# The second graph's channel sums turned on TensorE and laid in node order

## The chip, the core and the metric

The kernel runs on one core of a Trainium2 chip. The metric is the device time of one launch in microseconds (us). A core has five engines that work side by side, each through its own queue in program order: TensorE (PE; its weight loads are listed as PEld), VectorE (DVE), ScalarE (ACT), GpSimd (POOL) and SyncE (SP), which here only issues DMAs. Engines wait for one another by semaphores. All data are float32.

## The reference

Sixteen graphs of 1024 nodes with 256 channels share one adjacency matrix. Layer 0 normalises the nodes, weights the adjacency by the differences of the nodes' channel sums, and attends with what comes out as queries; layer 1 is a graph convolution with two batch norms. What matters here is the weighting:

```python
h = jnp.maximum(_layernorm(x, axis=-1), 0.0)
fea = jnp.transpose(h, (0, 2, 1))
c_adj = jnp.mean(fea, axis=1)
diff = c_adj[:, None, :] - c_adj[:, :, None]
A = jnp.abs(jnp.abs(jax.nn.sigmoid(diff) - 0.5) - 0.5) * 2.0
A_s = (A + jnp.transpose(A, (0, 2, 1))) * 0.5
Wg = adj[None, :, :] * A_s
g = jax.nn.relu(jnp.einsum('bcn,bnm->bcm', fea, Wg) * para.reshape(1, C, N))
# g gives the queries; h @ kv_w gives keys and values; 4 heads of 64
x = x + softmax_attention(q, k, v)
# layer 1: norm, adjacency aggregation, linear, batch norm, relu, linear, batch norm
```

`A_s[n, m]` depends only on the absolute difference of two nodes' channel sums: it is 1 - tanh(|difference of their means| / 2). So for each graph the kernel needs, for all pairs of nodes n (on partitions) and m (along the free dimension), the absolute difference of the sums, a tanh and a product with `adj`.

## The kernel before, in words

A graph's 1024 nodes are laid out as 8 tiles of 128 partitions (`P` = 128, `NT` = 8), node n = t * 128 + p. The channel sums of graph b, a by-product of the norm's relu (L341), lie in `csum`, 128 partitions by 8: partition p, column t. The weighting needs them also as a row of 1024 along the free dimension, the same on each partition. That row is `cbc`.

- `differences(b)` (from L401) makes `cbc`. For graph 0 it is made on chip (`columns_of` L201, `broadcast_row` L212 and L213), in the order of the nodes. For all other graphs `csum` is written to a DRAM buffer `csum_d` (L414) and read back as a broadcast to all partitions (L415), both on SP's queue. The write goes partition by partition, so `cbc` holds element p * 8 + t for node t * 128 + p, and a view with step 8 puts it right.
- `weigh(b)` then works through eight tiles `w` of 128 x 1024, each covering two node tiles and half of the m's: two ACTIVATEs (L450, absolute value of `csum` minus `cbc`, 512 elements each, read through the view of `cbc`), a tanh (L458) over the 1024, and a product with `adj` on DVE (L437). `adj` tiles are loaded by SP (L183) into a ring of three buffers.
- `transposed` (L396 and L399) turns the normalised nodes for the key and value products; `keys_values` (L171 as `pk` and `pv`, copies at L624 and L641) and `plain_queries` (L171 as `pg`, L604, L607) make keys, values and queries. `plain_queries` serves graphs 0 and 1. All these products, and the transposes, take turns in two PSUM banks (`bank`, tag `mm`).
- `attention` runs over all graphs in steps of two score tiles: scores (L882) into two PSUM buffers, an exponential (L890), the value products (L923) one step later, and sums of the exponentials on DVE (L909 and L912).

The order is written out by hand (`manual_schedule`). Between two attention steps of graph b, `attention` takes pieces from a generator, `background(b)`, as long as their costs stay below what is due by then. A piece is mostly one or two products with what belongs to them; the costs only steer how many pieces come after each step. Every engine runs its instructions in the order in which the pieces issue them. The background of graph 0 begins with `differences(1)`, issued after the scores and exponentials of step 0 and before those of step 1. Then come the transposes of graph 1 at the top of the next two steps, key products with the weighting of graph 1 woven in (two slots of weighting for each piece), the norm of graph 2, `plain_queries(1)`, and, from its fifth and seventh piece, `graph()` (GpSimd prepares seven combinations of the adjacency in DRAM, `aht_d`, for layer 1) and `degrees()` (L226 to L240, `at` tiles loaded by SP at L217 into the same three buffers as `adj`). After that `differences(2)` and the rest.

The background of the later graphs weights graph b + 1 or b + 2 beside the attention in the same way. The weighting of graph 0 is done before the attention begins.

The buffer `s1` (128 x 4 x 128, one copy) is used in `degrees()` for the masked diagonal (L234), and later for the sums of quarters in the queries and in layer 1.

Of the kernel before, what the change touches and what calls it, by code (L numbers as in the profile page):

```python
# [10 lines left out]
F32 = mybir.dt.float32  # L11
# [6 lines left out]
P = 128  # L18
# [5 lines left out]
def gnn_two_layers_kernel(  # L24
# [12 lines left out]
    nc = tc.nc  # L37
    B, N, C = x.shape
    H1 = w1_t.shape[1]
    NT = N // P  # L40
# [14 lines left out]
    ident = const.tile([P, P], F32, name="ident")  # L55
# [16 lines left out]
    csum_d = [dram.tile([N], F32, name=f"csum_d{b}") for b in range(B)]  # L72
# [23 lines left out]
    def layers(shifted):  # L96
# [9 lines left out]
        p1 = st.enter_context(tc.tile_pool(name=f"p1_{kind}", bufs=1))  # L106
# [15 lines left out]
        csums, cbcs, weighted, weighers = {}, {}, {}, {}  # L122
# [41 lines left out]
        def bank(name):  # L164
            return ps_mm.tile([P, FB], F32, tag="mm", name=name)
# [30 lines left out]
        def columns_of(col, name):  # L196

            cbs = []
            for g in range(NT // 4):
                cb = py.tile([P, 4, P], F32, tag="y", name=f"cb_{name}_{g}")  # L200
                nc.vector.tensor_copy(  # L201
                    cb, col[:, 4 * g : 4 * g + 4].unsqueeze(2).to_broadcast([P, 4, P])
                )
                cbs.append(cb)
            return cbs

        def broadcast_row(dst, cbs, name):

            for g, cb in enumerate(cbs):
                pt = bank(f"cbp_{name}_{g}")  # L210
                for j in range(4):
                    nc.tensor.transpose(pt[:, j * P : (j + 1) * P], cb[:, j, :], ident)  # L212
                nc.scalar.copy(dst[:, g * FB : (g + 1) * FB], pt)  # L213
# [8 lines left out]
        row, diag, col, deg, tmp_deg, dinv = (deg_sm[:, i, :] for i in range(6))  # L222
# [178 lines left out]
        def differences(b):  # L401


            cbc = p1.tile([P, N], F32, tag="cbc", name=f"cbc_{b}")
            cbcs[b] = (
                cbc.rearrange("p (t q) -> p t q", t=NT)
                if b == 0
                else cbc.rearrange("p (q t) -> p t q", t=NT)
            )
            weighers[b] = weigh(b)  # L410
            if b == 0:
                broadcast_row(cbc, columns_of(csums[b], f"c{b}"), f"c{b}")
                return
            nc.sync.dma_start(out=csum_d[b].rearrange("(p t) -> p t", p=P), in_=csums[b])  # L414
            nc.sync.dma_start(  # L415
                out=cbc, in_=csum_d[b].rearrange("(o n) -> o n", o=1).to_broadcast([P, N])
            )

        def weigh(b):


            csum, cbc = csums[b], cbcs[b]
            made = weighted[b] = []
            adjs = []

            def load():
                q, th = divmod(len(adjs), NP)
                adjs.append(load_adj(q, th, f"adj_{b}_{q}_{th}"))

            load()  # L430
            for slot in range(2 * NH * NP + 1):
                i, odd = divmod(slot, 2)
                q, th = divmod(i, NP)
                if not odd and i > 0:

                    w, a = made[i - 1], adjs[i - 1]
                    nc.vector.scalar_tensor_tensor(w, w, 1.0, a, op0=ALU.add, op1=ALU.mult)  # L437
                    if b == 0:
                        q, th = divmod(i - 1, NP)
                        nc.vector.tensor_reduce(  # L440
                            rows[:, q, th * TH : (th + 1) * TH], a, AX.X, ALU.add
                        )
                if not odd and i < NH * NP:
                    q, th = divmod(i, NP)
                    if i + 1 < NH * NP:
                        load()
                    w = p8.tile([P, TH, FB], F32, tag="w", name=f"w_{b}_{q}_{th}")
                    made.append(w)
                    for t in range(TH):
                        nc.scalar.activation(  # L450
                            w[:, t, :].rearrange("p (t q) -> p t q", q=P),
                            cbc[:, q * NT // NH : (q + 1) * NT // NH],
                            AF.Abs,
                            bias=csum[:, th * TH + t : th * TH + t + 1],
                            scale=-1.0,
                        )
                if odd:
                    nc.scalar.activation(made[i], made[i], AF.Tanh, scale=-0.5 / C)  # L458
                yield 0.0
# [307 lines left out]
        def summed(b):  # L767
            yield from Norm(b, True).all()
            differences(b)
            yield 0.0  # L770
# [15 lines left out]
        def background(b):  # L786

            if b == 0:
                differences(1)
                for k in range(CC):  # L790
                    yield TOP
                    transposed(1, k)
                    yield 1.0
                w, products, norm = weighers[1], keys_values(1), Norm(2, True).all()
                yield from weave(
                    islice(products, 4), (0, double(islice(w, 8))), (0, islice(norm, 4))
                )
                yield from weave(
                    plain_queries(1), (0, norm), (0, w), (5, graph()), (7, degrees())
                )  # L800
                differences(2)
                yield from islice(products, 2)
                yield from prepare(2, products)
                return
# [627 lines left out]
```

## Time and profile before

| | |
|---|---|
| time, median of 3 runs | 2615.71 us (2615.10 to 2615.84) |
| time of the profiled execution | 2615.69 us |
| span of the profiled execution, first to last instruction | 2613.6 us |
| mean granted TensorE clock | 0.990 |
| ScalarE busy | 1468.9 us of the span |
| L450, all graphs | 256 instructions, 293.7 us of ScalarE |
| write of the sums (L414), issue to landing | 1.4 us median, 1.4 to 7.4 |
| broadcast back (L415), issue to landing | 4.4 us median, 4.2 to 4.9 |

In a timeline each line has the start in us, the duration, engine, line, operation, what is written and read with its shapes, how many instructions were merged, and in brackets how long the engine stood idle before it and for whom. A shape such as 64*128 64x512 on a TensorE row is the stationary operand by the moving one. In the groups by line, busy us and mean ns of one instruction stand after the first bar, idle time after the second. Matmul ends are modelled, so short overlaps of neighbouring rows mean nothing.

### The profile page before, as it was taken

To read this page: it belongs to the slowest core of one execution; us is meant where nothing else is said; L and a number is where in the kernel's file an instruction comes from. 1 tells how busy PE (TensorE), PEld (TensorE's weight loads), DVE (VectorE), ACT (ScalarE), POOL (GpSimd) and SP (SyncE) were. 2 spreads that over 40 slices of the span, in tenths; PEclk is the share of its full clock that TensorE was granted. 3 is DMA by queue.
4 is the path that set the end of the run, shared out by engine and by line. 5 is a ranking of instruction groups with operands and counts; after the bars stand their busy time and mean duration, and the time that the engine had idled before them with its cause. 6 is when DMAs were issued, how large, how long until landed. Compare 5 with 4: busy or idle time off the path is not lost. (4 is left out here: it accounts for less than half of the span.)

```text
span 2613.6 us, 31371 instructions
## 1 busy us (share of the span) xinstructions
PE 2525.8 (97%) x11626; PEld 931.8 (36%) x11626; DVE 1824.7 (70%) x2837; ACT 1468.9 (56%) x2033; POOL 393.6 (15%) x456
## 2 busy tenths in 40 slices
PE   7899999999999999999999999999999999999994
PEld 3333333333333333333333333333333333334443
DVE  4668686767768686868677676868686766657774
ACT  6875564647474645656474747465565634335543
POOL 1550100010101001000001010000100001026653
PEclk9999999999999999999999999999999999999997
DMA  4554324152524342241524243433325242355459
GB/s 158 178 197 145 121 81 162 61 189 77 181 81 153 101 151 95 97 157 55 188 73 181 85 153 109 145 101 113 138 63 180 64 166 104 109 191 224 169 198 365
DMA packets 131043, 363.46 MB, mean 139 GB/s; under 512 B 15425, under 2 KB 32321, under 8 KB 124737
## 3 DMA queue, kind: packets, MB, share of 16 engines
q1 hardware_dynamic: 110272, 282.70, 31.5%
q0 software_dynamic: 20608, 78.66, 7.9%
q8 instruction: 94, 1.54, 0.3%
q14 instruction: 69, 0.56, 0.1%
HBM read 286.79 MB, written 74.51 MB: 138 GB/s over the span
## 5 line engine op out<-in xcount | busy, mean ns | idle before, releaser
L890 ACT ACTIVATE p<-sc 128x1024 f32<-128x1024 f32 x512 | 495.2, 1020 | 450.8 <-PE sc L882 450.3
L912 DVE TENSOR_TENSOR acc<-acc,p 128x1024 f32<-128x1024 f32 x384 | 472.4, 1230 | 144.7 <-ACT p L890 123.2
L882 PE MATMUL sc<-q,k 64*128 64x512 f32 x2048 | 509.0, 615 | 8.8 <-ACT p L890 8.8
L923 PE MATMUL o<-p,v 128*64 128x512 f32 x2048 | 495.9, 605 | 0.0
L171 PE MATMUL pg<-w,h_a 128*64 128x512 f32 x1600 | 357.9, 592 | 4.4 <-DVE q L604 2.5
L171 PE MATMUL pa<-aht,h_b 128*64 128x512 f32 x1536 | 345.4, 594 | 3.5 <-ACT h_b L341 3.4
L882 PEld LDWEIGHTS sc<-q,k 64*128 64x128 f32 x2048 | 175.8, 186 | 330.9 <-issue 285.4
L450 ACT ACTIVATE w<-cbc,csum 128x512 f32<-128x512 f32 x256 | 293.7, 1199 | 0.0
L171 PE MATMUL py<-at,w 128*64 128x512 f32 x1024 | 234.0, 600 | 8.4 <-ACT ht L399 7.1
L437 DVE SCALAR_TENSOR_TENSOR w<-w,adj 128x1024 f32<-128x1024 f32 x128 | 157.2, 1228 | 118.8 <-ACT w L458 114.6
L923 PEld LDWEIGHTS o<-p,v 128*64 128x64 f32 x2048 | 124.1, 136 | 250.3 <-issue 247.2
L171 PEld LDWEIGHTS pg<-w,h_a 128*64 128x64 f32 x1600 | 114.7, 137 | 233.2 <-issue 215.2
L738 POOL DMA_DIRECT2D y_d<-y x128 | 70.8, 553 | 797.3 <-ACT y L737 789.5
L171 PEld LDWEIGHTS pa<-aht,h_b 128*64 128x64 f32 x1536 | 111.2, 137 | 217.5 <-issue 208.9
L737 ACT ACTIVATE y<-py,vec 128x512 f32<-128x512 f32 x128 | 87.6, 684 | 143.5 <-PE py L171 120.4
L741 DVE BATCH_NORM_STATS2 stats<-y 128x6 f32<-128x512 f32 x128 | 85.6, 687 | 80.7 <-ACT y L737 80.6
L458 ACT ACTIVATE w<-w 128x1024 f32<-128x1024 f32 x128 | 135.2, 1056 | 1.7
L512 DVE TENSOR_TENSOR w<-w,w 128x1024 f32<-128x1024 f32 x112 | 132.8, 1216 | 1.5
L341 ACT ACTIVATE h_b<-x,lnsm_b 128x256 f32<-128x256 f32 x128 | 70.4, 608 | 110.7 <-DVE lnsm_b L330 110.7
L93 POOL TENSOR_SCALAR lnsm_b<-mv_b 128x4 f32<-128x4 f32 x32 | 12.2, 381 | 790.9 <-DVE mv_b L319 790.9
L171 PEld LDWEIGHTS py<-at,w 128*64 128x64 f32 x1024 | 72.5, 138 | 163.3 <-issue 130.8
L171 PE MATMUL pk<-ht,kvw_f 128*64 128x512 f32 x512 | 116.8, 599 | 2.5 <-ACT ht L399 1.5
(155 smaller groups left out, 2778.8 us busy)
## 6 DMA issues: line engine op xcount, KB each, us to landing
aht<-aht_d SPq DMA_DIRECT2D x224, 512.0 KB, 6.3
adj<-in_adj_dram SPq DMA_DIRECT2D x128, 512.0 KB, 4.5
y_d<-y POOLq DMA_DIRECT2D x128, 256.0 KB, 2.6
yin_f<-y_d SPq DMA_DIRECT2D x32, 1024.0 KB, 6.3
x<-in_x_dram SPq DMA_DIRECT2D x32, 512.0 KB, 5.2
para<-in_para_dram SPq DMA_DIRECT2D x64, 256.0 KB, 3.9
x_d<-x POOLq DMA_DIRECT2D x16, 1024.0 KB, 10.3
xo_f<-x_d SPq DMA_DIRECT2D x32, 512.0 KB, 8.2
```

Of the source, the lines that this page charges most:

```text
L171: nc.tensor.matmul(dst[r], left[:, r], right, start=start, stop=stop)
L437: nc.vector.scalar_tensor_tensor(w, w, 1.0, a, op0=ALU.add, op1=ALU.mult)
L450: nc.scalar.activation(w[:, t, :].rearrange("p (t q) -> p t q", q=P), cbc[:, q * NT // NH : (q + 1) * NT // NH], AF.Abs, bias=csum[:, th * ...
L458: nc.scalar.activation(made[i], made[i], AF.Tanh, scale=-0.5 / C)
L512: nc.vector.tensor_sub(block(i)[part], block(x)[part], block(y)[part])
L737: nc.scalar.activation(y, made, AF.Identity, bias=b1[:, j : j + 1])
L738: nc.gpsimd.dma_start(out=y1_d[i][:, j, :], in_=y)
L741: nc.vector.bn_stats(stats1[:, j, i, :], y)
L882: nc.tensor.matmul(sc[:, e, :], ks[b][k][r, m * P : (m + 1) * P], qs[b][k][r, f * FB : (f + 1) * FB], start=True, stop=True,)
L890: nc.scalar.activation(pr, sc, AF.Exp)
L912: nc.vector.tensor_add(self.acc, self.acc, pr)
L923: nc.tensor.matmul(self.o[r, :], vs[b][k][:, m, r], pr[:, e, :], start=(m == 0), stop=(m == NT - 1),)
```

## The change

Only graph 1 is treated differently, and only in `differences`. Its `csum` (128 x 8) is turned by TensorE into a PSUM bank as 8 x 128, copied by ScalarE to a row tile in the buffer `s1`, and this is written to `csum_d`, in eight runs of 128 floats, node by node. The broadcast back is the same instruction as before. The view of `cbc` is then the one of graph 0, with step one. Graphs 2 to 15 keep the old way.

```diff
             cbcs[b] = (
                 cbc.rearrange("p (t q) -> p t q", t=NT)
-                if b == 0
+                if b <= 1
                 else cbc.rearrange("p (q t) -> p t q", t=NT)
             )
...
-            nc.sync.dma_start(out=csum_d[b].rearrange("(p t) -> p t", p=P), in_=csums[b])
+            if b == 1:
+                turned = bank(f"csumt_{b}")[0:NT, 0:P]
+                nc.tensor.transpose(turned, csums[b], ident)
+                row = p1.tile([P, NT // 2, P], F32, tag="s1", name=f"csumr_{b}")[0:NT, 0, :]
+                nc.scalar.copy(row, turned)
+                nc.sync.dma_start(out=csum_d[b].rearrange("(t p) -> t p", p=P), in_=row)
+            else:
+                nc.sync.dma_start(out=csum_d[b].rearrange("(p t) -> p t", p=P), in_=csums[b])
             nc.sync.dma_start(
                 out=cbc, in_=csum_d[b].rearrange("(o n) -> o n", o=1).to_broadcast([P, N])
             )
```

The name `bank` takes the next of the two PSUM banks; the transpose takes one turn there.

## The prediction

> **What bounds the kernel now.** I read the page's busy shares first, then windows over stages, then the timelines of TensorE and ScalarE in the one stage that stands out.
>
> ```profile
> PE 2525.8 (97%) x11626; PEld 931.8 (36%) x11626; DVE 1824.7 (70%) x2837; ACT 1468.9 (56%) x2033; POOL 393.6 (15%) x456
> ```
>
> TensorE is busy for 97% of the span, so an edit that speeds another engine pays only where TensorE stands still for that engine. The windows (span, then busy time and instruction count of PE, PEld, DVE, ACT, POOL, then clock, DMA share, GB/s) say where that is:
>
> ```profile
> 60.00:105.00 45.00, 37.59 (x172) 12.54 (x170) 21.18 (x34) 37.98 (x53) 13.62 (x17) 1.00 0.46 141
> 105.00:170.00 65.00, 65.00 (x328) 24.50 (x328) 48.84 (x62) 42.60 (x60) 53.10 (x67) 1.00 0.73 253
> 170.00:200.00 30.00, 25.63 (x120) 8.93 (x118) 20.22 (x23) 27.82 (x33) 3.41 (x4) 1.00 0.36 101
> 200.00:600.00 400.00, 398.19 (x1910) 141.84 (x1908) 290.92 (x458) 224.64 (x318) 31.03 (x48) 1.00 0.37 127
> ```
>
> From 60 to 105 us TensorE loses 45.00 - 37.59 = 7.41 us; from 105 to 170 it loses nothing; afterwards some 4 us around 175, and under 2 us in each 400 us. The reader is to see that the only large stall of the first 600 us lies where graph 1 is weighted beside graph 0's attention. TensorE's timeline has the pieces of it:
>
> ```profile
> 64.29 2.04 PE L882 MATMUL sc<-q,k 64*128 64x512 f32 x8 [0.45 <-ACT p L890]
> 80.25 1.94 PE L171 MATMUL pk<-ht,kvw_f 128*64 128x512 f32 x8 [1.06 <-ACT k L624]
> 84.06 1.94 PE L171 MATMUL pg<-w,h_a 128*64 128x512 f32 x8 [1.88 <-ACT k L624]
> 95.52 2.04 PE L882 MATMUL sc<-q,k 64*128 64x512 f32 x8 [2.30 <-ACT p L890]
> 102.86 2.04 PE L882 MATMUL sc<-q,k 64*128 64x512 f32 x8 [1.71 <-ACT p L890]
> ```
>
> All five wait for ScalarE; the last four sum to 6.95 us. ScalarE's timeline shows why:
>
> ```profile
> 75.80 0.59 ACT L624 COPY k<-pk 128x512 f32<-128x512 f32 x1 [2.56 <-PE pk L171]
> 76.28 2.35 ACT L450 ACTIVATE w<-cbc,csum 128x512 f32<-128x512 f32 x2
> 78.66 1.06 ACT L458 ACTIVATE w<-w 128x1024 f32<-128x1024 f32 x1
> ...
> 99.56 2.34 ACT L450 ACTIVATE w<-cbc,csum 128x512 f32<-128x512 f32 x2
> 101.79 1.92 ACT L890 ACTIVATE p<-sc 128x1024 f32<-128x1024 f32 x2
> ...
> 118.52 1.94 ACT L890 ACTIVATE p<-sc 128x1024 f32<-128x1024 f32 x2 [1.26 <-PE sc L882]
> ```
>
> No bracket with idle time stands between 75.80 and 118.52: ScalarE is the bound there, and eight pairs of L450, 2.31 to 2.38 us each, lie in that stretch. They all belong to graph 1. The groups by shape, first from 20 to 60 us (graph 0), then from 58 to 200 us (graphs 1 and 2):
>
> ```profile
> L450 ACT ACTIVATE w<-cbc,csum 128x512 f32<-128x512 f32 x16 | 10.6, 717 | 0.0
> ```
> ```profile
> L450 ACT ACTIVATE w<-cbc,csum 128x512 f32<-128x512 f32 x28 | 33.0, 1231 | 0.0
> ```
>
> The same instruction takes 717 ns for graph 0 and 1231 ns for the others. Graph 0's view of `cbc` has step one; the others' view `(q t)` walks it with a step of eight floats, 32 bytes.
>
> [...] L396 shows 272. [...] the sums' write landed in 1.4 us for graph 1.
>
> **The change part by part.** *The new view* makes graph 1's sixteen L450 read with step one. I take graph 0's duration. By starts, a pair followed by the tanh (L458) takes 2.38 now (76.28 to 78.66) and 1.35 for graph 0 (35.44 to 36.79): 1.03 saved. A pair followed by another instruction takes 2.21 to 2.23 now and 1.24 for graph 0 (23.44 to 24.68): 0.98 saved. ScalarE saves some 8.2 us, of which TensorE can keep no more than the 6.95 us it lost. Stall by stall:
>
> The fourth key product (80.25) waits for the second key copy to free its bank. One pair lies before that copy, so it may start at 80.25 - 1.03 = 79.22; TensorE is free at 79.19. The stall of 1.06 becomes 0.03. The first query product (84.06) waits for the third copy, two pairs on: 84.06 - 2.06 = 82.00. TensorE is free at 79.22 + 1.93 = 81.15, so 0.85 of the 1.88 remains. Gain so far 2.06. The scores at 95.52 wait for an exponential behind five pairs: ScalarE permits 95.52 - (4 x 1.03 + 0.98) = 90.42. TensorE's work before it ended at 93.22 and now ends at 93.22 - 2.06 = 91.16, which is later: the 2.30 goes, gain 4.36. The scores at 102.86 are behind six pairs: ScalarE permits 102.86 - 6.08 = 96.78, TensorE is ready at 101.15 - 4.36 = 96.79. The 1.71 goes and the gain is 6.07, a tie that can leave a tenth. After it TensorE is the bound until 173; the remaining two pairs save ScalarE time only.
>
> Is something else late? The first weight product L437 (79.75) follows the tanh and moves to 78.7, so does the norm of graph 2 woven between: its last shift waits for GpSimd behind the third L437 and its statistics, and comes at about 87.9 instead of 90.97. ScalarE wants its result first in the third pair of L341, at about 93, after the 87.9. The first pair, at 91.09 - 4.12 = 86.97, needs only the earlier shift (85.60, now about 83.5). GpSimd's graph work, queued behind that norm, starts 3 us earlier and not 6; its product is first read by the `aht` load at 239.73, and it ends at 171. The `at` tiles that ScalarE reads from 120 on are loaded when DVE frees a buffer, so they move with DVE; ScalarE waited 1.75 us for one at 138.6, but the scores after it want its exponential only at 145.4. Nothing there reaches TensorE.
>
> *The transpose* stands in TensorE's queue between the scores of step 0, ending at 63.84, and those of step 1, waiting until 64.29 for an exponential. The sums are complete at 57.95, the bank was last read at 60.94. At 272 ns it fits in the 0.45 us gap: I take 0; without the cover 0.3.
>
> *The copy of 8 x 128* stands on ScalarE between the exponentials of steps 0 and 1. No trace row shows it. L641 (256 elements, 375 ns) and L399 (512, 586 ns) point to 0.27 us[...]. ScalarE idles 0.31 there (65.47). At most 0.1 us is pushed on the next exponential, which TensorE awaits only at 69.16: 0.
>
> *The DMAs.* The write keeps its size, with 8 runs of 512 bytes in place of 128 of 32, so 1.4 us or less; its issue moves from 57.97 to about 65.5. Behind it on SP's queue wait the broadcast (59.39, now about 67.0) and three loads of `adj` (59.76, now about 67.3). Nothing else is passed. The broadcast took 4.5 us to land: 71.5, needed at 76.28. The three loads ended about 8.5 us after the broadcast's issue, by the rate of transfer in that stretch: 75.5, the first needed at 78.7. Both fit: cost 0, with 4.8 and 3 us of slack. The fourth load waits for the first L437 as before. The row takes the buffer `s1`, next written at 124.8, when its write has long landed.
>
> Sum: -6.07 + 0 to 0.3; I take -6.0. The profiled execution took 2615.69 us, its span 2613.6 and 2.09 around it; span 2607.6, time 2609.7. The median of the runs, 2615.71, is the same within 0.02, so no correction.
>
> **The rivals.** *The query-bank wait goes as well*, or the tie falls well: all 6.95 us come back, 2608.7. Against it: the third copy stands behind two tanh and two pairs, and those stay. *Given back later*: the gain at 105 us meets a transfer or GpSimd's work that moves only 3 us, and some 3 us return, 2612.7. For it: DMA share 0.73 from 105 to 170 and waits for DMA there. Against it: the slack above. *No effect*: the slow read is caused by something other than the step, such as the tile being filled by DMA; then 2615.7 plus 0 to 0.3, 2615.8. Against it is the equality of all else in L450. *Slower*: the broadcast is late. Graph 2's pair, in a busy stretch, took 7.4 us to write and 4.9 to read; from 65.5 that lands at 77.8, 1.5 us late, which still leaves a gain of some 4.5. The change loses once write and broadcast together take over about 17 us (10.8 to reach 76.28, plus 6 of gain); at 22 us, 2615.7 - 6 + 11.2 = 2620.9. Against it: the engines of DMA are almost still from 53 to 59 us, and nothing new is queued before.
>
> **How the numbers follow.** The forecast 0.72, all back 0.08, given back 0.10, no effect 0.05, slower 0.05. Range: 2608.5 (all back, with a few tenths between runs) to 2611.7 (forecast with the transpose uncovered, the tie lost and a part of the giving back). 0.2% of 2615.7 is 5.2 us, about what a measurement here tells from no change, so faster means below 2610.5: all of the second case, nearly nine tenths of the first, 0.71. Same: the rest of the first, the third and the fourth, 0.24. Slower 0.05.
>
> **What would show it.** Right: graph 1's L450 at about 717 ns; stalls at 79.2, 91.2 and 96.8 gone, one of about 0.85 left before the first query product near 82; TensorE's later work 6 us earlier all the way; the broadcast issued near 67. Wrong: L450 still above 1.2 us, ScalarE waiting for `cbc` near 76, a new TensorE stall between 62 and 66, or the 105 to 170 window no longer full.

## The result, and the profile after

The changed kernel takes 2609.47 us (median of 12 runs, 2606.23 to 2610.26) against 2615.16 us for the kernel before (12 runs, 2614.34 to 2616.09). The ratio is 0.9976, with a 95% interval from 0.9969 to 0.9984: 5.7 us faster. The prediction said 2609.7.

The windows of the changed kernel, with the same columns as before. The third stretch is the former 105 to 170, moved by the 6 us by which everything behind the stage now comes earlier:

```profile
60.00:105.00 45.00, 43.75 (x199) 14.71 (x197) 26.97 (x38) 37.44 (x62) 16.57 (x20) 1.00 0.50 161
60.00:99.00 39.00, 37.75 (x173) 12.59 (x171) 21.50 (x33) 32.34 (x56) 10.67 (x14) 1.00 0.50 156
99.00:164.00 65.00, 65.00 (x330) 24.61 (x328) 46.46 (x63) 40.61 (x59) 54.89 (x72) 1.00 0.75 262
164.00:194.00 30.00, 25.64 (x122) 8.90 (x120) 20.48 (x24) 27.79 (x33) 2.84 (x2) 1.00 0.34 93
```

TensorE loses 45.00 - 43.75 = 1.25 us from 60 to 105, where it lost 7.41. The next 65 us are full as before, and the 4.4 us around graph 2 stay. Its timeline in the stage:

```profile
63.54 0.27 PE L417 MATMUL csumt<-ident,csum 128*8 128x128 f32 x1
64.06 2.04 PE L890 MATMUL sc<-q,k 64*128 64x512 f32 x8 [0.25 <-ACT p L898]
...
73.63 7.30 PE L171 MATMUL pk<-ht,kvw_f 128*64 128x512 f32 x32
81.79 1.94 PE L171 MATMUL pg<-w,h_a 128*64 128x512 f32 x8 [0.86 <-ACT k L632]
...
90.88 1.99 PE L890 MATMUL sc<-q,k 64*128 64x512 f32 x8
...
96.55 2.03 PE L890 MATMUL sc<-q,k 64*128 64x512 f32 x8
```

The four key products now run as one piece of 32 records; of the four stalls of 6.95 us only the one at the first query product is left. The line numbers are 8 higher behind the change (L450 is now L458, the scores L882 are L890, the exponential L890 is L898). ScalarE's timeline, and the group of graph 1's reads between 58 and 135 us:

```profile
64.81 0.24 ACT L419 COPY csumr<-csumt 8x128 f32<-8x128 f32 x1
65.23 1.94 ACT L898 ACTIVATE p<-sc 128x1024 f32<-128x1024 f32 x2 [0.19 <-PE sc L890]
...
76.05 1.33 ACT L458 ACTIVATE w<-cbc,csum 128x512 f32<-128x512 f32 x2
...
104.99 1.94 ACT L898 ACTIVATE p<-sc 128x1024 f32<-128x1024 f32 x2 [0.86 <-PE sc L890]
```
```profile
L458 ACT ACTIVATE w<-cbc,csum 128x512 f32<-128x512 f32 x16 | 10.7, 719 | 0.0
```

A pair takes 1.33 us in place of 2.35. ScalarE's unbroken stretch, which ended at 117.3 before (its next exponential started at 118.52 after a wait of 1.26), ends at 104.1: from there it waits for TensorE.

All of the gain arises there and nothing of it is lost for the next 2000 us. SP issues the last graph's write of the sums at 1987.17 us against 1993.51 before: 6.34 us earlier. First before, then with the change:

```profile
1993.51 0.32 SPq L414 DMA_DIRECT2D csum_d<-csum  x1
```
```profile
1987.17 0.32 SPq L422 DMA_DIRECT2D csum_d<-csum  x1
```

Of this, 0.23 lay between the two executions at 64 us already (64.06 against 64.29). The stage gave 6.11. Behind that mark this one profiled execution is a further 3.0 us shorter, with a span of 2604.3 us against 2613.6; the last section says where most of that comes from.

### The profile page after: what moved, and what is told of

Its sections match the earlier page's. It is cut to its first block, busy times and chain, and to the rows that moved or that the text cites. A ratio compares the mean times of both kernels' runs of the same rounds, so it can differ in the third digit from the quotient of the medians.

```text
span 2604.3 us, 31375 instructions
## 1 busy us (share of the span) xinstructions
PE 2525.9 (97%) x11627; PEld 931.8 (36%) x11627; DVE 1822.7 (70%) x2837; ACT 1460.7 (56%) x2034; POOL 391.3 (15%) x456
## 4 chain that ended last, share of the span: by engine, by line
PE 87%; ACT 7%; DMA 2%; issue 2%; DVE 1%; SPq 0%; POOL 0%; POOLq 0%; DVEq 0%; ACTq 0%
PE sc L890 17%; PE o L931 16%; PE pa L171 15%; PE pg L171 14%; PE py L171 8%; PE m_f L1235 7%; PE pk L171 4%; PE pv L171 4%; ACT w L458 3%; DMA out_dram<-xo_f 2%; ACT p L898 2%; PE ot L986 1%; ACT w L466 1%; PE sums L961 1%; ACT ht L399 1%
## 5 line engine op out<-in xcount | busy, mean ns | idle before, releaser
L898 ACT ACTIVATE p<-sc 128x1024 f32<-128x1024 f32 x512 | 495.0, 1020 | 452.5 <-PE sc L890 452.1
L890 PE MATMUL sc<-q,k 64*128 64x512 f32 x2048 | 509.0, 615 | 4.7 <-ACT p L898 4.6
L890 PEld LDWEIGHTS sc<-q,k 64*128 64x128 f32 x2048 | 175.9, 186 | 325.5 <-issue 284.4
L458 ACT ACTIVATE w<-cbc,csum 128x512 f32<-128x512 f32 x256 | 285.5, 1168 | 0.0
L341 ACT ACTIVATE h_b<-x,lnsm_b 128x256 f32<-128x256 f32 x128 | 70.4, 609 | 110.7 <-DVE lnsm_b L330 110.7
```

Of the source, the lines that this page charges most:

```text
L458: nc.scalar.activation(w[:, t, :].rearrange("p (t q) -> p t q", q=P), cbc[:, q * NT // NH : (q + 1) * NT // NH], AF.Abs, bias=csum[:, th * ...
L890: nc.tensor.matmul(sc[:, e, :], ks[b][k][r, m * P : (m + 1) * P], qs[b][k][r, f * FB : (f + 1) * FB], start=True, stop=True,)
L898: nc.scalar.activation(pr, sc, AF.Exp)
```

## The experiments

Twelve runs, each compared with the kernel before on the same chip. The first four take the change apart.

**The turn with the old view.**

```diff
             cbcs[b] = (
                 cbc.rearrange("p (t q) -> p t q", t=NT)
-                if b <= 1
+                if b == 0
```

> Turn, copy and node-order write are kept, but graph 1 is read with the old view of step eight, so its weights belong to other nodes. Theory A (the step of the read is the cost, the added work is hidden): graph 1's L450 back at about 1.23 us, the four TensorE stalls of 6.95 us in all back, 2615.2 us plus 0 to 0.3. Rival B (the gain comes from the write in eight runs or from another order of the buffers and waits): about 2609.5 as with the change.

2615.04 us, ratio 0.9997 (0.9989 to 1.0006). Graph 1's reads:

```profile
L458 ACT ACTIVATE w<-cbc,csum 128x512 f32<-128x512 f32 x16 | 18.8, 1229 | 0.0
```

The tile is filled by the same broadcast, from a buffer written in the same way as with the change, and only the view differs: 1229 against 719 ns. So the step is the cost, and the write in eight runs alone brings nothing. The three stalls of 1.06, 1.88 and 2.31 us are back. Behind the third, TensorE ran slower for a while:

```profile
95.56 3.60 PE L890 MATMUL sc<-q,k 64*128 64x512 f32 x8 [2.31 <-ACT p L898]
```

The kernel before has 2.04 us for these eight score records after the same pause. That used up most of the time that TensorE would have waited a fourth time, so the fourth stall is 0.16 only. Expected were all four stalls; the time came out the same.

**The view alone** (the edit is shown against the change).

```diff
-            if b == 1:
-                turned = bank(f"csumt_{b}")[0:NT, 0:P]
...
-            else:
-                nc.sync.dma_start(out=csum_d[b].rearrange("(p t) -> p t", p=P), in_=csums[b])
+            nc.sync.dma_start(out=csum_d[b].rearrange("(p t) -> p t", p=P), in_=csums[b])
```

> The turn, the copy and the new write are left out; the old write stays and graph 1 is read with step one, so its weights belong to other nodes. Theory A: 2609.5 us within 0.4, the same stall of about 0.86 left, L450 at 0.71 us. Rival B: 2615.2. Rival C (the added work does cost TensorE or ScalarE something): below the change by more than 0.5, so 2609.0 or less.

2609.19 us, ratio 0.9974 (0.9963 to 0.9985): the same as the change within the intervals, with the same 0.86 us left at the first query product. The added turn, copy and later write cost nothing that can be measured; the next run, which has them, took 2609.04 us on the same chip.

**Six of eight pairs.**

```diff
-                            cbc[:, q * NT // NH : (q + 1) * NT // NH],
+                            (stepped if b == 1 and i >= 6 else cbc)[
+                                :, q * NT // NH : (q + 1) * NT // NH
+                            ],
```

> As with the change, but the last two of graph 1's eight pairs are read with step eight, so these weights belong to other nodes. Theory A: only the first six pairs count, because TensorE is the bound after the scores at 96.6; ScalarE is busy 2.1 us more, the time stays at 2609.5 within 0.4. Rival D (every pair counts alike): a quarter of the gain of 5.7 is lost, 2610.9.

2609.04 us, ratio 0.9977 (0.9967 to 0.9986). (`stepped` is the view of the same `cbc` with step eight, `i` the number of the pair from 0 on.) The last two pairs take 1.25 us an instruction again and TensorE's queue does not notice: from the scores at 64 to those at 104 us it takes 39.76 us, and 39.75 with the change. The last quarter of the 8.2 us that ScalarE saved buys TensorE nothing.

**The write in single floats, no turn** (against the kernel before; the view has `b <= 1` as in the change).

```diff
-            nc.sync.dma_start(out=csum_d[b].rearrange("(p t) -> p t", p=P), in_=csums[b])
+            order = "(t p) -> p t" if b <= 1 else "(p t) -> p t"
+            nc.sync.dma_start(out=csum_d[b].rearrange(order, p=P), in_=csums[b])
```

> No turn and no copy: the sums are written from their 128 partitions straight into node order, 1024 single floats. Theory A: only the order in memory matters and there is slack before the broadcast is needed; by the wait for the like write of dinv in the run before (10.8 us from 188.6) it lands near 69, the broadcast near 73.3, 3 us before it is needed: 2609.5 within 0.4. Rival E (the write is too slow): past 17 us of write and broadcast from 58 the first L450 starts late, up to 2615.

2608.61 us, ratio 0.9973 (0.9963 to 0.9984), 0.9 us below what was expected. The stage is not the reason: it takes TensorE 39.75 us, as with the change; three of the eight executions are short ones of 2606.4 to 2607.2 us, as the change has them too. The DMA issues from 50 to 80 us (the last number is the time to landing):

```profile
cbc<-csum_d SPq DMA_DIRECT2D x1, 512.0 KB, 6.2
csum_d<-csum SPq DMA_DIRECT2D x1, 4.0 KB, 8.4
```

The write of 1024 single floats takes 8.4 us and not the 1.4 of the kernel before, but it starts 7 us earlier than in the change, when the sums are ready and not when a turn and a copy have passed. The broadcast is issued at 66.46 us, where the change issues it at 66.32. So the engine work of the change isn't needed, and the next runs take this way further.

**Graphs 1 and 2 in that way** (`b <= 2` in both places).

> As the run with the scattered write, and graph 2 in the same way. Theory A: the two stalls of TensorE behind graph 2's first pairs (2.43 and 1.92 us) shrink to about 0.43 and 0.9, by two and three pairs of 1.0 us on ScalarE: 3.0 us less, 2606.0. Rival D (ScalarE's relief pays as such): 8 us less. Rival E (the write, issued at 133 us into busy DMA queues, makes the broadcast late for the 160.8 us at which it is read): no gain or a loss.

2606.52 us, ratio 0.9966 (0.9954 to 0.9978). What is left of graph 2's two stalls in TensorE's timeline:

```profile
165.34 2.04 PE L884 MATMUL sc<-q,k 64*128 64x512 f32 x8 [0.39 <-ACT p L892]
171.39 2.04 PE L884 MATMUL sc<-q,k 64*128 64x512 f32 x8 [0.90 <-ACT p L892]
```

They were 2.43 and 1.92, expected 0.43 and 0.9: the way of counting pairs ahead of a waiting instruction holds a second time.

**All graphs in that way** (the conditions hold for every graph from 1 on).

> All graphs from 1 on are written as single floats into node order and read with step one. ScalarE is relieved of another 107 us (13 graphs of 8.2). Theory A: no stall of TensorE waits for ScalarE's weighting there, so nothing more is gained than with graphs 1 and 2: 2606.0 within 0.6. Rival D: several us less for each graph, below 2590.

2592.27 us, ratio 0.9911 (0.9898 to 0.9925). It beats both kernels, by 23 and 17 us, and the expectation was wrong: 14.3 us more than with two graphs. Neither the theory nor the rival had it: it is 1.1 us a graph, not none and not 8. From the issues of the sums' writes, a graph of the middle takes 142.85 us in the kernel before, 142.84 with two graphs and 141.77 here; times 13 graphs (3 to 15) the difference is the 14 us. The groups of the second layer's products, first before and then here:

```profile
L171 PE MATMUL py<-at,w 128*64 128x512 f32 x1024 | 234.0, 600 | 8.4 <-ACT ht L399 7.1
```
```profile
L171 PE MATMUL py<-at,w 128*64 128x512 f32 x1024 | 232.7, 597 | 0.0
```

In the later graphs the products `py` wait for the copies of the turned nodes (L399) to free a bank, and these stand on ScalarE behind pairs of L450. One such place of the kernel before, TensorE first, then ScalarE:

```profile
594.48 1.94 PE L923 MATMUL o<-p,v 128*64 128x512 f32 x8
596.96 5.37 PE L171 MATMUL py<-at,w 128*64 128x512 f32 x24 [0.54 <-ACT ht L399]
```
```profile
592.24 2.37 ACT L450 ACTIVATE w<-cbc,csum 128x512 f32<-128x512 f32 x2
594.50 1.93 ACT L890 ACTIVATE p<-sc 128x1024 f32<-128x1024 f32 x2
596.31 1.08 ACT L399 COPY ht<-htp 128x512 f32<-128x512 f32 x2
```

The bracket shows 0.54 us, and the page of the whole profile sums 7.1 over 13 such places. The starts show more: elsewhere the next product starts 1.77 us after an L923 group, here 2.48 us after it, so 0.71 is lost; the second such place of the graph, where no bracket stands, loses 0.26. Together that is 0.97 of the 1.08. The ends of matmuls are modelled, and part of a stall hides under them. In this run both places have 1.77 us again (L923 is L925 here):

```profile
583.38 1.94 PE L925 MATMUL o<-p,v 128*64 128x512 f32 x8
585.15 5.32 PE L171 MATMUL py<-at,w 128*64 128x512 f32 x24
```

**The turn for all graphs** (`if b >= 1`, step one for every graph, the row in a buffer of the ring `y`).

> All graphs from 1 on take the turn on TensorE, the copy and the write in eight runs (the row lies in a buffer of its own ring). Theory A: TensorE is full from graph 2 on, so there each turn is paid in full, 0.27 us: 14 of them 3.8 us, against 3.0 from graph 2's stalls if its broadcast comes in time: 2610.3; graph 2's row is made only at about 149 us, and with 7.4 and 4.9 us of transfers comes 1 us late, so up to 2612. Rival D: faster than the change by tens of us.

2615.14 us, ratio 1.0001 (0.9992 to 1.0009), slower than expected by some 3 to 5 us. TensorE's waits:

```profile
PE pv L171 <- ACT csumr L419: 10.2, 1, 10.2
...
PE pa L171 <- ACT csumr L419: 4.5, 13, 0.3
```

The 10.2 us are a fault of the experiment: the ring `y` is also GpSimd's while it prepares the adjacency, so graph 2's copy waited 11.3 us for a tile of GpSimd's, and TensorE for the copy. The second line is the lesson. In the middle of the kernel a turn costs more than its 0.27 us: it takes one of the two banks, and the product behind it waits 0.34 us for ScalarE to empty it. A graph takes 142.53 us, 0.77 more than with single floats; turn and wait are 0.61 of that, and the rest is not explained. It is still 0.32 less than in the kernel before, so the turn for all graphs is worse than single floats but not useless: without the 10.2 us it would have taken, by an estimate from these runs, some 2605 us. Only the stall that hid it at 64 us made the turn free in the change.

**The change again**, unaltered.

> The change itself, unaltered, for its profile and times on this chip: 2609.5 within 0.5 for the median. If the lower clock after TensorE's two late pauses (near 2200 and 2285) comes and goes between executions, this profile may show it where the first one did not, with a span near 2607.5 instead of 2604.3.

2609.63 us, ratio 0.9978 (0.9970 to 0.9986); the span of its profile is 2607.9 us.

**Which pairs count in the later graphs.** Two runs divide the gain of the all-graphs version: from graph 3 on, step eight where `stepped` is chosen.

```diff
-                            cbc[:, q * NT // NH : (q + 1) * NT // NH],
+                            (stepped if b >= 3 and i >= 3 else cbc)[
+                                :, q * NT // NH : (q + 1) * NT // NH
+                            ],
```

> All graphs scattered as in the run before, but from graph 3 on only the first three of the eight pairs are read with step one, the other five with step eight (these weights belong to other nodes). Theory F (in the later graphs TensorE loses 1.08 us a graph because the copies of the turned nodes, for which the second layer's products wait, stand on ScalarE behind the first three pairs): 2592.3 us within 0.6, a period of 141.77 us a graph. Rival G (the five pairs beside the query products count): 2606.5, or something between.

> The counterpart: from graph 3 on only the last five pairs are read with step one, the first three with step eight (these weights belong to other nodes). ScalarE is relieved of 5 us a graph. Theory F: nothing of it reaches TensorE, 2606.5 within 0.6, period 142.84 us. Rival G: near 2592.3.

(The second has `i < 3`.) The first gives 2592.51 us, ratio 0.9909 (0.9896 to 0.9923), with 141.77 us a graph; the second 2604.63, ratio 0.9958 (0.9945 to 0.9972), with 142.86. TensorE between 600 and 1800 us, in the first and in the second:

```profile
600.00:1800.00 1200.00, 1200.00 (x5766) 430.24 (x5764) 877.05 (x1364) 679.91 (x976) 92.05 (x141) 1.00 0.36 121
```
```profile
600.00:1800.00 1200.00, 1194.75 (x5702) 424.70 (x5702) 873.61 (x1353) 654.17 (x960) 90.79 (x141) 1.00 0.35 118
```

The second has less work on ScalarE and the slower graphs. Three pairs bring all of the 1.08 us, five bring none. The starts at the two places of a graph agree: the `py` products follow after 1.76 us in the first run, after 2.49 and 2.05 us in the second. So it is the copies behind the first three pairs. The second run's median is 1.9 us below what was expected of it. Its graphs do not explain that: behind the last graph's write of its sums its profile takes 618.9 us, and that of the run with two graphs, which it should equal, 620.6. The last section shows that executions of one kernel differ there.

**Late broadcasts.** Two runs send graph 1's row through DRAM twice and three times (`range(2)` in the second).

```diff
                 nc.sync.dma_start(out=csum_d[b].rearrange("(t p) -> t p", p=P), in_=row)
+                for _ in range(1):
+                    nc.sync.dma_start(
+                        out=cbc, in_=csum_d[b].rearrange("(o n) -> o n", o=1).to_broadcast([P, N])
+                    )
+                    nc.sync.dma_start(out=csum_d[b].rearrange("(t p) -> t p", p=P), in_=row)
```

> The change, with graph 1's sums written, broadcast, written again and broadcast again. The second broadcast is issued at about 72.3 us and lands at 76.9, where the first read of it is due at 76.05. If the slack of 5 us that the prediction stated is right, 0.3 to 0.9 us are lost: 2610.1. If there is more slack than that: 2609.5; if less, because the adj loads behind it come late: 2612 or more.

> As before with two more trips: the last broadcast lands at about 82.8 us, 6.7 late. The prediction's case of a slower kernel: the whole chain on ScalarE moves by that and TensorE with it, 2616.2, slower than the kernel before by about 1. If TensorE has other work to put there, 2613 or less.

Once more gives 2609.09 us, ratio 0.9973 (0.9961 to 0.9984): no loss. A trip takes 4.6 to 4.8 us here, not the 5.9 that I had taken, and the second broadcast, issued at 70.75, was in time. Twice more gives 2613.69, ratio 0.9993 (0.9985 to 1.0001). There the wait is seen, first on ScalarE and then on TensorE:

```profile
80.32 1.33 ACT L463 ACTIVATE w<-cbc,csum 128x512 f32<-128x512 f32 x2 [4.18 <-DMA cbc<-csum_d]
```
```profile
83.27 3.68 PE L171 MATMUL pk<-ht,kvw_f 128*64 128x512 f32 x8 [4.33 <-ACT k L637]
```

The lateness of 4.3 us passes to TensorE. The records behind the pause ran slow (the granted clock from 60 to 105 us is 0.92, with the change 1.00): by their starts these eight took 1.6 us more than usual and the next eight 0.5. Against that, the stall of 0.86 at the query product and some tenths of others fell away. In sum the scores that the change starts at 103.81 start at 109.03, 5.2 us later; the medians of the two kernels lie 4.2 apart. The last broadcast was issued 9.3 us later than in the change and its first reader started 4.3 later, so the slack was about 5.1 us, where the prediction had 4.8.

## Why the prediction was right

- **The step of the read is the cost.** Predicted 717 ns an instruction, measured 719. Shown by the turn with the old view and by the view alone. Why a read with step eight takes longer (1229 to 1231 ns) was not shown: no run here tried another step.
- **The stalls, one by one.** With 0.23 us added for the offset at 64 us: first query product at 82.02, predicted 82.00; scores at 91.11, predicted 91.16; scores at 96.78, predicted 96.79. The stall that was to stay at 0.85 is 0.86. The stage gave 6.11 us, predicted 6.07. That the median, too, came within 0.2 us of 2609.7 is in part luck: executions of the change range from 2606.23 to 2610.26, and the last section shows a difference at the kernel's end that the prediction did not treat.
- **The last two pairs bring nothing to TensorE.** Shown by the run with six.
- **The turn and the copy are hidden.** 0.27 and 0.24 us, in gaps of 0.45 and 0.31. What is left of these gaps in the timeline is 0.25 and 0.19. The 0.1 us that the prediction allowed on the next exponential was its author's estimate; none of it is seen: the exponential starts at 65.23, and 65.47 less the offset of 0.23 is 65.24. Shown by the view alone, which is no faster; the all-graphs turn shows what they cost without the cover, 0.77 us a graph, where the prediction had put 0.3 for the transpose.
- **The DMAs are in time.** The broadcast was issued at 66.32, predicted about 67.0: 1.25 us behind the write at 65.07, where the kernel before has 1.42. One more trip is absorbed, two are not.
- **Nothing takes the gain back.** GpSimd's graph work started at 87.59 us, 3.3 earlier, as the prediction said, and TensorE was as full from 99 to 164 as before. The rival that saw part of the gain returned there falls.
- **The rival on the other side**, a late broadcast, had the right mechanism, and its case did not arise. Its sum lets the change lose once write and broadcast together take over about 17 us. With two more trips they took about 15.2 (65.06 to 80.3), and the kernel ended 2.0 us under the one before, with an interval that includes no difference. That a longer delay makes a loss follows from the sum and was not run.

Two readings did not decide this change, but were wrong for the kernel. The stall in graph 1 is not the only large one of the first 600 us: the windows shown begin at 60, and before that TensorE stands still for 13.3 us, 8.8 of them before its first instruction. And "under 2 us in each 400 us" of the later windows was taken as busy enough. With 1.08 us a graph it was 3.0 us in each 400 and 14 us in all, twice what the change was after, and it stood in the page as 7.1 us behind L399.

## What to carry to other kernels

Count what stands on an engine's queue ahead of the one instruction that the bound engine waits for, not the engine's busy time: of 8.2 us saved in graph 1 six pairs counted, in the later graphs three of eight. A small stall that repeats with each pass is found by the period of a mark (here the issue of the sums' write), better than by the idle time before TensorE's matmuls, whose modelled ends cover part of it (here a bracket of 0.54 us where the starts lose 0.97). Where data has time to spare, let a DMA put it in order, slow as it is (8.4 us for the single floats), rather than engines that have none.

## What the runs showed of the hardware

In some executions a pause of TensorE cost time twice. Near the kernel's end TensorE has the same pause of 2.74 us in eleven of the fourteen profiles; the other three were not read there. The eight matmul records behind it, in the change's first profile and in its second:

```profile
2198.37 1.94 PE L171 MATMUL pa<-aht,h_b 128*64 128x512 f32 x8 [2.74 <-ACT h_b L341]
```
```profile
2198.92 3.58 PE L171 MATMUL pa<-aht,h_b 128*64 128x512 f32 x8 [2.74 <-ACT h_b L341]
```

This is one kernel, and the two are 1.6 us apart. The granted clock from 2195 to 2205 us is 1.00 in the first profile and 0.83 in the second. If all that is missing there lies in these records, they had a clock of about 0.53 (0.17 of 10 us over 3.58 us); that is an estimate. The kernel before takes 3.32 us for the same eight, at a clock of 0.58. A second pause, of 4.96 and 4.97 us and 80 us further on, adds 1.3: from its end to the start of the next product that waits for L341, at 2291.09 or 2294.59 us, it takes 12.43 us in the first and 13.73 in the second. Together that is most of the 3.6 us between the two spans, and the kernel before, whose profile has 13.61 us at the second place, is to be compared with the second. The length of the pause alone does not decide it: behind the 2.74 us the clock fell in the second profile and not in the first. In the run with the old view it fell behind 2.31 us (0.96 from 60 to 105 us, the score records in 3.60 us), and in the kernel before 2.30 us at the same place cost nothing (2.04 us, at a clock of 1.00). What decides it in an execution was not tried.
